# A message-passing kernel: edge groups of 125 with 12 targets in place of 250 with 24, and one of four source one-hots on ScalarE

## The chip, the cores and the metric

The kernel runs on one core of a Trainium2 chip. The core has five engines with a queue of instructions each: TensorE (PE, matmuls; its weight loads have a row of their own, PEld), VectorE (DVE), ScalarE (ACT), GpSimd (POOL) and SyncE (SP, which here only starts transfers). They wait for each other through semaphores. The metric is the time of one execution on the device in microseconds, as a median of several runs; one further execution is recorded by the profiler.

## The reference

The inputs are x of 1250 nodes with 1024 features, 40,000 edges (src, dst) sorted by target, two graph layers, and a mixture of eight experts. Cut to what matters:

```python
def sage_layer(h, src, dst, deg_inv, W_self, W_neigh, b):
    agg = segment_sum(h[src], dst, num_segments=N)
    return h @ W_self + (agg * deg_inv[:, None]) @ W_neigh + b

deg = segment_sum(ones, dst, N);  deg_inv = 1 / maximum(deg, 1)
h = relu(sage_layer(layernorm(x), ..., W_self0, W_neigh0, b0))
x = x + sage_layer(h, ..., W_self1, W_neigh1, b1)
x = x + ffn(layernorm(x))     # router, top 2 of 8 experts, weighted sum
```

The targets are drawn as 1250 u^2 with u uniform, so they are denser at low numbers.

## The kernel before

The sum over edges is a matrix product: C[s, t] is the number of edges from source s to target t, and agg = C^T h. C is kept on the chip as 10 blocks of 128 sources by 1250 targets (`C`, line 367, fp32r). Both layers multiply by it; its column sums are the degrees.

**How C is counted.** The 40,000 edges, in the order given, are cut into 160 groups of 250. As targets are sorted, a group has few different targets; the kernel assumes at most 24 (`WIN`), numbered from the group's first. A group is two subgroups of 125 edges (`GC, GP`), one edge on each partition. For a subgroup, a one-hot of the source's low seven bits is made on GpSimd (`ol`, line 413, 125 x 128), a one-hot of the pair (source block, target within the window) on VectorE (`oh`, line 420, 125 x 240), and a matmul of the two (line 423) counts the edges; the two subgroups of a group accumulate in PSUM. The 240 counts are then added on VectorE (line 442) to the ten block rows of C at the group's first target. That place is known only at run time: line 437 loads it into a VectorE register ahead of each addition, and register arithmetic makes an address of it (also recorded under line 442).

**Rows of groups.** Two groups (four subgroups) are a row; there are 80. `row_of_groups` makes the four `ol`, then four times `oh` and matmul into one PSUM tile (`cnt`, three buffers), and then, when more than two rows are open, `close_row` makes the two additions of the oldest. `oh` and `ol` have six buffers each. `make_keys` and `turn_keys` compute and transpose the numbers that the one-hots compare with; `turn_ranges` brings first and last target of each group to one partition; `verdict` tests that every group fits its window (if not, a general path runs after everything else, which these inputs don't take).

**What lies around it.** While C is counted, TensorE multiplies the normalised tokens by `W_self0` (`self_unit`, line 462, evicted by ScalarE on line 466) and by `W_neigh0` (`y_unit`, line 528; `split`, lines 393 and 394, evicts with one ScalarE copy and one VectorE subtraction). `some_groups(n)` puts n rows of groups between the units: 9 rows before the loop, 2, 4 and 4 before the three units of each of six blocks, 1 before each of ten y units, and the rest behind them. The first matmul that reads the finished C is line 553 (degrees); then come the products with C (line 564).

**What sets the order.** The opening (LayerNorm of six blocks, transposes, first units, keys) is written out by hand for VectorE, ScalarE and TensorE (`manual_schedule`). Elsewhere a planner simulates the engines and takes, for each, the earliest instruction in program order that is ready; `keep_in_program_order` pins an instruction behind the one traced before it on its engine. Once planned, each engine's queue is fixed, and its instructions start in that order.

Of the kernel before, what the change touches and what calls it, by code (L numbers as in the profile page):

```python
# [10 lines left out]
F32 = mybir.dt.float32  # L11
F32R = mybir.dt.float32r
F16 = mybir.dt.float16
# [7 lines left out]

P = 128
EPS = 1e-5
WIN = 24
GC, GP = 2, 125
LQ = 32


# [1 line left out]
def kernel(  # L30
# [28 lines left out]
    QW = D // 4  # L59
    NB = -(-N // P)  # L60
    NP = NB * P
    EG = GC * GP
    NGR = NE // EG
    R = NGR // 2
    WEXP = KD * H + KH * D
    NTILE = (2 * N) // P + E
    assert R * 2 * EG == NE and R <= P and 2 * NB * WIN <= 512 and N > WIN
    rows = [min(P, N - b * P) for b in range(NB)]

    step = -(-(N - 2 * P) // 4) * 2  # L70
# [72 lines left out]
    stt = nc.vector.scalar_tensor_tensor  # L143


    RE = 2 * EG
    assert 8 * RE <= 4000 and 3 * NGR <= 500 and 8480 + 6 * NGR <= 9440
# [16 lines left out]
    nc.vector.memset(eps, EPS)  # L164

    nc.scalar.activation(small.tile([P, 1], F32, name="rs"), eps, AF.Sqrt)
    ident = const.tile([P, P], F32, name="ident")
    make_identity(nc, ident)

# [27 lines left out]
    nc.scalar.dma_start(out=b0_p, in_=b0.rearrange("(k p) -> p k", p=P))  # L197


    ext = const.tile([R, 3, 2], F32, name="ext")  # L200
    base_i = const.tile([1, NGR], I32, name="base_i")

    keys = const.tile([GP, 2, 2 * GC, R], F32, name="keys")
# [4 lines left out]
    APART = 16  # L208
    assert APART * EG < 4096

    dst_halves = dst_f.rearrange("p (a n) -> p a n", a=2)

    def make_keys():

        nc.vector.tensor_reduce(ext[:, 0, :], dst_halves, AX.X, ALU.min)
        nc.vector.tensor_scalar(ext[:, 2, :], ext[:, 0, :], float(N - WIN), None, op0=ALU.min)
        nc.vector.tensor_scalar(hi_i, src_i, 7, None, op0=ALU.arith_shift_right)
        nc.vector.tensor_scalar(lo_i, src_i, P - 1, None, op0=ALU.bitwise_and)
        nc.vector.tensor_copy(hi_f, hi_i)
        nc.vector.tensor_copy(lo_f, lo_i)  # L220
        stt(key, hi_f, float(WIN), dst_f, op0=ALU.mult, op1=ALU.add)
        for i in range(2):
            part = key[:, i * EG : (i + 1) * EG]
            nc.vector.tensor_scalar(part, part, ext[:, 2, i : i + 1], None, op0=ALU.subtract)

    def turn_keys():
        for a, v in enumerate((key, lo_f)):
            ps = tpp.tile([P, 4, P], F32, name="tp")
            pf = ps.rearrange("p a b -> p (a b)")
            for c in range(2 * GC):  # L230
                nc.tensor.transpose(
                    pf[:GP, c * R : (c + 1) * R], v[:, c * GP : (c + 1) * GP], ident[:R, :R]
                )
            nc.scalar.copy(keys[:, a].rearrange("p c g -> p (c g)"), pf[:GP, : 2 * GC * R])

    def turn_ranges():

        nc.vector.tensor_reduce(ext[:, 1, :], dst_halves, AX.X, ALU.max)
        for a in (2, 0, 1):
            pe = tpp.tile([P, 4, P], F32, name="tp")  # L240
            for i in range(2):
                nc.tensor.transpose(pe[:1, i, :R], ext[:, a, i : i + 1], ident[:R, :R])
            nc.vector.tensor_copy(
                gx[:, a, :].rearrange("o (r i) -> o i r", i=2), pe[:1, :2, :R]
            )
            if a == 2:
                nc.vector.tensor_copy(base_i, gx[:, 2, :])

    def verdict():

        bad = L[:1, 8480 : 8480 + 6 * NGR].rearrange("o (a g) -> o a g", a=6)
        nc.vector.memset(bad, -1.0)
        stt(bad[:, 0, :], hi_, float(1 - WIN), lo_, op0=ALU.add, op1=ALU.subtract)
        nc.vector.tensor_tensor(bad[:, 1, : NGR - 1], lo_[:, : NGR - 1], lo_[:, 1:], ALU.subtract)
        nc.vector.tensor_tensor(bad[:, 2, : NGR - 1], hi_[:, : NGR - 1], hi_[:, 1:], ALU.subtract)
        stt(
            bad[:, 3, : NGR - APART], hi_[:, : NGR - APART], 1.0, lo_[:, APART:],
            op0=ALU.add, op1=ALU.subtract,
        )
# [97 lines left out]
    def gnn_windows():  # L357
# [26 lines left out]

        yh = yp.tile([P, NB, QW], F32R, name="yh")
        yl = yp.tile([P, NB, QW], F32R, name="yl")
        win = yp.tile([P, NB * WIN], F16, name="win")
        win_i = yp.tile([P, NB * WIN], I32, name="win_i")
        nc.gpsimd.iota(win_i, pattern=[[1, NB * WIN]], base=0, channel_multiplier=0)
# [18 lines left out]
        GW = NB * WIN  # L408

        def row_of_groups(r):  # L410
            ol = hot.tile([GP, 2 * GC, P], F16, name="ol")
            for c in range(2 * GC):
                nc.gpsimd.tensor_scalar(  # L413
                    ol[:, c, :], lane[:GP], keys[:, 1, c, r : r + 1], None, op0=ALU.is_equal
                )
            ps = pc.tile([P, 2, 256], F32, name="cnt")
            for i in range(2):
                for c in range(GC):
                    oh = hot.tile([GP, GW], F16, name="oh")
                    nc.vector.tensor_scalar(  # L420
                        oh, win[:GP], keys[:, 0, i * GC + c, r : r + 1], None, op0=ALU.is_equal
                    )
                    nc.tensor.matmul(  # L423
                        ps[:, i, :GW], ol[:, i * GC + c, :], oh,
                        start=(c == 0), stop=(c == GC - 1),
                    )
            open_rows.append((r, ps))
            if len(open_rows) > 2:
                close_row()

        open_rows = []

        def close_row():
            r, ps = open_rows.pop(0)
            for i in range(2):
                g = 2 * r + i
                at = nc.values_load(
                    base_i[0:1, g : g + 1], engines=(ENG.DVE,), min_val=0, max_val=N - WIN,
                    skip_runtime_bounds_check_because="cut at N - WIN, and a target is never below 0",
                )  # L440
                to = C[:, :, ds(at, WIN)]
                nc.vector.tensor_tensor(  # L442
                    to, to.bitcast(F32),
                    ps[:, i, :GW].rearrange("p (k w) -> p k w", k=NB), ALU.add,
                )

        groups = iter(range(R))

# [87 lines left out]
        for q in range(4):  # L536
            w_q = w_next
            w_next = load_q(w_neigh0, q + 1) if q < 3 else None
            for b in range(NB):
                if q == 0:  # L540
                    some_groups(1)
                y_unit(w_q, h0T, b, yh[: rows[b], b, :], yl[: rows[b], b, :])
            if q == 3:
                w_half = load_half(w_neigh1, 0)
            if q == 0:
                some_groups(R)
                while open_rows:
                    close_row()

                for c0, n in cchunks:  # L550
                    ps = mm.tile([P, 512], F32, name="ps")
                    for k in range(NB):
                        nc.tensor.matmul(
                            ps[:, :n], ones_r, C[:, k, c0 : c0 + n],
                            start=(k == 0), stop=(k == NB - 1),
                        )
                    nc.vector.tensor_scalar(dinv[:, c0 : c0 + n], ps[:, :n], 1.0, None, op0=ALU.max)
                    nc.vector.reciprocal(dinv[:, c0 : c0 + n], dinv[:, c0 : c0 + n])
# [1123 lines left out]
```

## Time and profile before

| | |
|---|---|
| median of 3 runs | 1146.44 us (1146.19 to 1147.84) |
| profiled execution, its own time | 1146.48 us |
| its span | 1144.3 us |
| granted TensorE clock, mean | 0.993 |
| TensorE busy | 1108.3 us |
| VectorE, GpSimd, ScalarE busy | 451.1, 331.7, 181.5 us |
| counting stage, first one-hot to the first matmul on the finished C | 31.64 to 234.62 us |

A group of instructions in the profile is one line, engine and operation: out<-in by tile names, partitions x elements, count, busy time and mean of one in ns; behind the bar the engine's idle time just before them and who ended it. In a row of stretches each engine has its busy time and in brackets the number of instructions. In a timeline a row is start, length, engine, line and operation, merged over neighbours. Register instructions (DVEq) are not counted as busy.

### The profile page before, as it was taken

The numbers are of one execution on the slowest core, as the hardware profiler recorded it, in microseconds if no ns is written. First come the engines' busy times: TensorE is split into PE (matmuls) and PEld (weight loads), VectorE is DVE, ScalarE is ACT, GpSimd is POOL, SyncE is SP. The second block draws the span as 40 slices with busy tenths as digits, with TensorE's granted clock in tenths as the row PEclk, the third lists the DMA queues.
The fourth block names the chain that finished last, engine by engine and source line by source line (L and its number), as shares of the span: only waits on it lengthen the run. The fifth ranks groups of instructions, "written<-read, shape, count | busy, mean of one in ns | idle before, by whom it ended". The sixth has DMA issues, their size and how long they took to land.

```text
span 1144.3 us, 13214 instructions
## 1 busy us (share of the span) xinstructions
PE 1108.3 (97%) x4775; PEld 791.2 (69%) x4775; DVE 451.1 (39%) x1129; ACT 181.5 (16%) x420; POOL 331.7 (29%) x438
## 2 busy tenths in 40 slices
PE   6999999999999999999999999999999989999994
PEld 4556556888888886887688778885444766666662
DVE  8777777761212154341224132555322542111110
ACT  5301000001111111100110000123011223222220
POOL 1899999800000000032003002342000013223221
PEclk9999999999999999999999999999999999999997
DMA  6110111010100021042004261335921435444542
GB/s 230 34 38 5 38 38 38 1 37 1 38 1 1 1 74 38 1 154 93 7 10 168 88 222 42 117 148 209 373 60 37 150 92 136 112 113 105 127 115 45
DMA packets 59330, 95.40 MB, mean 83 GB/s; under 512 B 8797, under 2 KB 35645, under 8 KB 59251
## 3 DMA queue, kind: packets, MB, share of 16 engines
q1 hardware_dynamic: 48400, 67.72, 17.3%
q0 software_dynamic: 7056, 23.88, 9.2%
q10 hardware_dynamic: 3798, 2.84, 0.8%
q8 instruction: 42, 0.69, 0.2%
q14 instruction: 34, 0.28, 0.1%
HBM read 68.76 MB, written 27.47 MB: 84 GB/s over the span
## 4 chain that ended last, share of the span: by engine, by line
PE 93%; DVE 2%; ACT 1%; DMA 1%; POOL 1%; issue 0%; ACTq 0%; DVEq 0%; POOLq 0%
PE ps L528 12%; PE ps L462 11%; PE psb L642 9%; PE ps L712 8%; PE ps L564 8%; PE ps L642 7%; PE ps L1516 7%; PE ps L1541 7%; PE ps L1188 5%; PE ps L629 5%; PE ps L1202 4%; PE cnt L423 3%; PE tp L1504 2%; PE ps L1141 2%; PE ps L1537 1%; PE tp L322 1%
## 5 line engine op out<-in xcount | busy, mean ns | idle before, releaser
L413 POOL TENSOR_SCALAR ol<-lane,keys 125x128 f16<-125x128 f16 x320 | 193.2, 622 | 27.6 <-DVE oh L420 27.6
L462 PE MATMUL ps<-h0T,L 128*128 128x498 f32 (+2 forms) x384 | 147.4, 518 | 0.2 <-ACT h0T L325 0.2
L528 PE MATMUL ps<-L,h0T 128*128 128x256 f32 (+1 forms) x640 | 142.0, 380 | 0.0
L708 POOL TENSOR_TENSOR L<-L 128x512 f32<-128x512 f32 (+1 forms) x20 | 31.4, 1576 | 375.1 <-DMA L<-in_L_gnn_b_dram 216.5
L528 PEld LDWEIGHTS ps<-L,h0T 128*128 128x128 f32 (+1 forms) x640 | 118.7, 188 | 17.7 <-issue 0.5
L420 DVE TENSOR_SCALAR oh<-win,keys 125x240 f16<-125x240 f16 x320 | 84.7, 322 | 32.7 <-PE cnt L423 31.1
L462 PEld LDWEIGHTS ps<-h0T,L 128*128 128x128 f32 x384 | 68.1, 192 | 38.3 <-issue 33.9
L1516 PE MATMUL ps<-xw,L 128*128 x368 | 84.9, 384 | 0.4 <-issue 0.4
L1541 PE MATMUL ps<-xw,L 128*128 x184 | 83.5, 597 | 0.1
L564 PE MATMUL ps<-C,yh 128*128 128x256 f32 (+2 forms) x240 | 81.9, 356 | 0.0
L564 PE MATMUL ps<-C,yl 128*128 128x256 f32 (+2 forms) x240 | 81.5, 354 | 0.0
L712 PE MATMUL ps<-zh,C 128*128 128x512 f32 (+1 forms) x200 | 79.6, 398 | 0.0
L712 PE MATMUL ps<-zl,C 128*128 128x512 f32 (+1 forms) x200 | 78.7, 393 | 0.0
L1516 PEld LDWEIGHTS ps<-xw,L 128*128 128x128 f32 x368 | 69.2, 193 | 10.3 <-issue 1.8
L1552 POOL DMA_INDIRECT out_dram<-L x23 | 36.3, 1579 | 133.5 <-ACT L L1505 87.9
L442 DVE TENSOR_TENSOR C<-C,cnt 128x240 f32 x160 | 64.3, 402 | 12.5 <-DVE oh L420 1.6
L1493 POOL DMA_INDIRECT L<-t_d,L x26 | 26.0, 1000 | 148.1 <-DVE L L141 127.8
L1541 PEld LDWEIGHTS ps<-xw,L 128*128 128x128 f32 x184 | 33.3, 190 | 35.3 <-issue 32.9
L423 PEld LDWEIGHTS <-ol 125*128 125x128 f16 x320 | 30.9, 97 | 36.7 <-POOL ol L413 20.0
L1549 DVE TENSOR_SCALAR L<-ps,L 128x512 f32<-128x512 f32 x23 | 17.3, 751 | 91.8 <-PE ps L1541 91.8
L394 DVE TENSOR_TENSOR yl<-ps,yh 128x256 fp32r<-128x256 f32 (+1 forms) x40 | 16.9, 424 | 92.1 <-ACT yh L393 92.1
L423 PE MATMUL cnt<-oh,ol 125*128 125x240 f16 x320 | 50.0, 266 | 2.6 <-POOL ol L413 2.1
(226 smaller groups left out, 1504.3 us busy)
## 6 DMA issues: line engine op xcount, KB each, us to landing
xw<-in_L_ffn_ew_dram SPq DMA_DIRECT2D x16, 1024.0 KB, 7.6
L<-in_x_dram SPq DMA_DIRECT2D x20, 256.0 KB, 2.8
v_d<-L SPq DMA_DIRECT2D x18, 256.0 KB, 2.0
xa<-v_d SPq DMA_DIRECT2D x18, 256.0 KB, 6.0
t_d<-L SPq DMA_DIRECT2D x9, 512.0 KB, 4.0
out_dram<-xa SPq DMA_DIRECT2D x9, 512.0 KB, 3.7
L<-in_L_gnn_W_self_dram SPq DMA_DIRECT2D x4, 1024.0 KB, 5.4
L<-in_L_gnn_W_neigh_dram SPq DMA_DIRECT2D x4, 1024.0 KB
```

The costliest lines, as they stand in the source:

```text
L413: nc.gpsimd.tensor_scalar(ol[:, c, :], lane[:GP], keys[:, 1, c, r : r + 1], None, op0=ALU.is_equal)
L420: nc.vector.tensor_scalar(oh, win[:GP], keys[:, 0, i * GC + c, r : r + 1], None, op0=ALU.is_equal)
L423: nc.tensor.matmul(ps[:, i, :GW], ol[:, i * GC + c, :], oh, start=(c == 0), stop=(c == GC - 1),)
L442: nc.vector.tensor_tensor(to, to.bitcast(F32), ps[:, i, :GW].rearrange("p (k w) -> p k w", k=NB), ALU.add,)
L462: nc.tensor.matmul(ps[:, :n], w[:, k, (d % 2) * P : (d % 2 + 1) * P], h0T[:, k, c0 : c0 + n], start=(k == 0), stop=(k == KD - 1),)
L528: nc.tensor.matmul(ps[:m, :QW], hT[:, k, blk(b)], w[:, k, :], start=(k == 0), stop=(k == KD - 1))
L564: nc.tensor.matmul(ps[:, :n], part[: rows[k], k, (d % 2) * P : (d % 2 + 1) * P], C[: rows[k], k, c0 : c0 + n], start=(k == 0 and part is y ...
L629: nc.tensor.matmul(ps[:m], hT1[:, k, blk(b)], w[:, k, :], start=(k == 0), stop=(k == KD - 1))
L642: nc.tensor.matmul(ps, rows_of(k), w[:, k, :], start=(first and k == 0), stop=(k == KB - 1), skip_group_check=not first,)
L712: nc.tensor.matmul(ps[:m], C[: rows[k], k, blk(b)], part[: rows[k], k, :], start=(k == 0 and part is yh), stop=(k == NB - 1 and part is yl),)
L1516: nc.tensor.matmul(ps[:, :H], xT[:, k, :], w1_all[:, ds(e, 1), k * H : (k + 1) * H], start=(k == 0), stop=(k == KD - 1),)
L1541: nc.tensor.matmul(ps, hT[:, q, :], w2_all[:, ds(e, 1), q * D + h * HALF : q * D + (h + 1) * HALF], start=False, stop=(q == KH - 1),)
```

## The change

- A group is 125 edges with at most 12 targets (`EG`, `WIN`); a row is four groups (`RG`), still 80 rows. The two subgroups no longer share a result: each of the four matmuls of a row writes 120 counts of its own, and there are 320 additions of 120 counts, each with its register load.
- `row_of_groups` makes three source one-hots on GpSimd; the fourth comes from ScalarE as relu(1 - |key - lane|) in two activations.
- Additions no longer follow a row in a block: after each one-hot and matmul, `add_group` makes one addition once eight groups are waiting. One-hots and additions are pinned in program order on VectorE.
- `ext`, `base_i` and `keys` move from the pool that lives throughout to one that is freed after the stage; the verdict's scratch is twice as long and lies over the edge words (4000 on) rather than behind the ranges. The ranges are 320 numbers instead of 160, so their turn needs four transposes where it had two.
- 16 matmuls of the identity with itself, whose result nobody reads, stand at the head of TensorE's order.
- Two rows instead of one precede the first y unit.

```diff
-WIN = 24
-GC, GP = 2, 125
+WIN = 12
+EG = 125
+RG = 4
...
-    R = NGR // 2
+    R = NGR // RG
...
-    RE = 2 * EG
+    RE = RG * EG
...
+    one_p = const.tile([P, 1], F32, name="one_p")
+    nc.vector.memset(one_p, 1.0)
...
-        for i in range(2):
+        for i in range(RG):
             part = key[:, i * EG : (i + 1) * EG]
             nc.vector.tensor_scalar(part, part, ext[:, 2, i : i + 1], None, op0=ALU.subtract)
...
         for a in (2, 0, 1):
             pe = tpp.tile([P, 4, P], F32, name="tp")
-            for i in range(2):
+            for i in range(RG):
                 nc.tensor.transpose(pe[:1, i, :R], ext[:, a, i : i + 1], ident[:R, :R])
...
-        bad = L[:1, 8480 : 8480 + 6 * NGR].rearrange("o (a g) -> o a g", a=6)
+        bad = L[:1, 4000 : 4000 + 6 * NGR].rearrange("o (a g) -> o a g", a=6)
...
         def row_of_groups(r):
-            ol = hot.tile([GP, 2 * GC, P], F16, name="ol")
-            for c in range(2 * GC):
-                nc.gpsimd.tensor_scalar(
-                    ol[:, c, :], lane[:GP], keys[:, 1, c, r : r + 1], None, op0=ALU.is_equal
-                )
-            ps = pc.tile([P, 2, 256], F32, name="cnt")
-            for i in range(2):
-                for c in range(GC):
-                    oh = hot.tile([GP, GW], F16, name="oh")
+            ol = hot.tile([EG, RG, P], F16, name="ol")
+            for i in range(RG):
+                k = keys[:, 1, i, r : r + 1]
+                if i < RG - 1:
+                    nc.gpsimd.tensor_scalar(ol[:, i, :], lane[:EG], k, None, op0=ALU.is_equal)
+                else:
+
+                    away = hot.tile([EG, P], F16, name="away")
+                    nc.scalar.activation(away, lane[:EG], AF.Abs, scale=-1.0, bias=k)
+                    nc.scalar.activation(ol[:, i, :], away, AF.Relu, scale=-1.0, bias=one_p[:EG])
+            ps = pc.tile([P, RG, P], F32, name="cnt")
+            for i in range(RG):
+                oh = hot.tile([EG, GW], F16, name="oh")
+                tc.keep_in_program_order(
                     nc.vector.tensor_scalar(
-                        oh, win[:GP], keys[:, 0, i * GC + c, r : r + 1], None, op0=ALU.is_equal
+                        oh, win[:EG], keys[:, 0, i, r : r + 1], None, op0=ALU.is_equal
                     )
-                    nc.tensor.matmul(
-                        ps[:, i, :GW], ol[:, i * GC + c, :], oh,
-                        start=(c == 0), stop=(c == GC - 1),
-                    )
-            open_rows.append((r, ps))
-            if len(open_rows) > 2:
-                close_row()
...
+                )
+                nc.tensor.matmul(ps[:, i, :GW], ol[:, i, :], oh, start=True, stop=True)
+
+                if len(to_add) >= 2 * RG:
+                    add_group()
+            to_add.extend((r, ps, i) for i in range(RG))
+
+        to_add = []
+
+        def add_group():
+            r, ps, i = to_add.pop(0)
+            g = RG * r + i
+            at = nc.values_load(
+                base_i[0:1, g : g + 1], engines=(ENG.DVE,), min_val=0, max_val=N - WIN,
...
+            to = C[:, :, ds(at, WIN)]
+            tc.keep_in_program_order(
                 nc.vector.tensor_tensor(
                     to, to.bitcast(F32),
                     ps[:, i, :GW].rearrange("p (k w) -> p k w", k=NB), ALU.add,
                 )
+            )
...
+            idle = mm.tile([P, 512], F32, name="ps")
+            for _ in range(16):
+                nc.tensor.matmul(idle[:, :P], ident, ident, start=True, stop=True)
             step(0, 0, 1, 0, 1)
...
-                    some_groups(1)
+                    some_groups(2 if b == 0 else 1)
...
-                while open_rows:
-                    close_row()
+                while to_add:
+                    add_group()
```

More of the change, by code (lines that the diff above doesn't have):

```diff
@@ L61 @@
     NP = NB * P
-    EG = GC * GP
     NGR = NE // EG
-    R = NGR // 2
+    R = NGR // RG
     WEXP = KD * H + KH * D
     NTILE = (2 * N) // P + E
-    assert R * 2 * EG == NE and R <= P and 2 * NB * WIN <= 512 and N > WIN
+    assert R * RG * EG == NE and R <= P and RG * NB * WIN <= 512 and N > WIN
     rows = [min(P, N - b * P) for b in range(NB)]
@@ L143 @@
     stt = nc.vector.scalar_tensor_tensor
-    RE = 2 * EG
-    assert 8 * RE <= 4000 and 3 * NGR <= 500 and 8480 + 6 * NGR <= 9440
+    RE = RG * EG
+    assert 8 * RE <= 4000 and 3 * NGR <= 1440 and 6 * NGR <= 4 * RE
     edge = L[:R, 4000:8000].rearrange("p (a n) -> p a n", n=RE)
@@ L197 @@
     nc.scalar.dma_start(out=b0_p, in_=b0.rearrange("(k p) -> p k", p=P))
-    ext = const.tile([R, 3, 2], F32, name="ext")
-    base_i = const.tile([1, NGR], I32, name="base_i")
-    keys = const.tile([GP, 2, 2 * GC, R], F32, name="keys")
+    ext = base_i = keys = None
     worst = const.tile([1, 1], F32, name="worst")
@@ L207 @@
     lo_, hi_ = gx[:, 0, :], gx[:, 1, :]
-    APART = 16
+    APART = 32
     assert APART * EG < 4096
-    dst_halves = dst_f.rearrange("p (a n) -> p a n", a=2)
+    dst_groups = dst_f.rearrange("p (a n) -> p a n", a=RG)
     def make_keys():
-        nc.vector.tensor_reduce(ext[:, 0, :], dst_halves, AX.X, ALU.min)
+        nc.vector.tensor_reduce(ext[:, 0, :], dst_groups, AX.X, ALU.min)
         nc.vector.tensor_scalar(ext[:, 2, :], ext[:, 0, :], float(N - WIN), None, op0=ALU.min)
@@ L229, in turn_keys @@
             pf = ps.rearrange("p a b -> p (a b)")
-            for c in range(2 * GC):
+            for c in range(RG):
                 nc.tensor.transpose(
-                    pf[:GP, c * R : (c + 1) * R], v[:, c * GP : (c + 1) * GP], ident[:R, :R]
+                    pf[:EG, c * R : (c + 1) * R], v[:, c * EG : (c + 1) * EG], ident[:R, :R]
                 )
-            nc.scalar.copy(keys[:, a].rearrange("p c g -> p (c g)"), pf[:GP, : 2 * GC * R])
+            nc.scalar.copy(keys[:, a].rearrange("p c g -> p (c g)"), pf[:EG, : RG * R])
     def turn_ranges():
-        nc.vector.tensor_reduce(ext[:, 1, :], dst_halves, AX.X, ALU.max)
+        nc.vector.tensor_reduce(ext[:, 1, :], dst_groups, AX.X, ALU.max)
         for a in (2, 0, 1):
             pe = tpp.tile([P, 4, P], F32, name="tp")
-            for i in range(2):
+            for i in range(RG):
                 nc.tensor.transpose(pe[:1, i, :R], ext[:, a, i : i + 1], ident[:R, :R])
             nc.vector.tensor_copy(
-                gx[:, a, :].rearrange("o (r i) -> o i r", i=2), pe[:1, :2, :R]
+                gx[:, a, :].rearrange("o (r i) -> o i r", i=RG), pe[:1, :, :R]
             )
@@ L386, in gnn_windows @@
         yl = yp.tile([P, NB, QW], F32R, name="yl")
+        nonlocal ext, base_i, keys
+        ext = yp.tile([R, 3, RG], F32, name="ext")
+        base_i = yp.tile([1, NGR], I32, name="base_i")
+        keys = yp.tile([EG, 2, RG, R], F32, name="keys")
         win = yp.tile([P, NB * WIN], F16, name="win")
@@ L410, in row_of_groups @@
         def row_of_groups(r):
-            ol = hot.tile([GP, 2 * GC, P], F16, name="ol")
-            for c in range(2 * GC):
-                nc.gpsimd.tensor_scalar(
-                    ol[:, c, :], lane[:GP], keys[:, 1, c, r : r + 1], None, op0=ALU.is_equal
-                )
-            ps = pc.tile([P, 2, 256], F32, name="cnt")
-            for i in range(2):
-                for c in range(GC):
-                    oh = hot.tile([GP, GW], F16, name="oh")
-                    nc.vector.tensor_scalar(
-                        oh, win[:GP], keys[:, 0, i * GC + c, r : r + 1], None, op0=ALU.is_equal
-                    )
-                    nc.tensor.matmul(
-                        ps[:, i, :GW], ol[:, i * GC + c, :], oh,
-                        start=(c == 0), stop=(c == GC - 1),
-                    )
@@ L427, in row_of_groups @@
-            open_rows.append((r, ps))
-            if len(open_rows) > 2:
-                close_row()
[L431 to L441, printed above, removed]
+            ol = hot.tile([EG, RG, P], F16, name="ol")
@@ new lines, in row_of_groups @@
+            for i in range(RG):
+                oh = hot.tile([EG, GW], F16, name="oh")
+                tc.keep_in_program_order(
+                    nc.vector.tensor_scalar(
+                        oh, win[:EG], keys[:, 0, i, r : r + 1], None, op0=ALU.is_equal
+                    )
+                )
+                nc.tensor.matmul(ps[:, i, :GW], ol[:, i, :], oh, start=True, stop=True)
+                if len(to_add) >= 2 * RG:
+                    add_group()
+            to_add.extend((r, ps, i) for i in range(RG))
@@ L442, in close_row @@
+        to_add = []
[4 more added lines that the diff above has]
+                base_i[0:1, g : g + 1], engines=(ENG.DVE,), min_val=0, max_val=N - WIN,
+                skip_runtime_bounds_check_because="cut at N - WIN, and a target is never below 0",
+            )
+            to = C[:, :, ds(at, WIN)]
+            tc.keep_in_program_order(
                 nc.vector.tensor_tensor(
@@ L445, in close_row @@
                 )
+            )
         groups = iter(range(R))
```

## The prediction

> **What bounds the kernel now.** I read the page first, then busy time by stretch, the groups, the waits and the timeline of the stretch that the change touches.
>
> ```profile
> PE 1108.3 (97%) x4775; PEld 791.2 (69%) x4775; DVE 451.1 (39%) x1129; ACT 181.5 (16%) x420; POOL 331.7 (29%) x438
> ```
>
> TensorE is busy 97% of the span, so a microsecond counts if it comes off TensorE or makes TensorE wait. The stretches of the counting stage:
>
> ```profile
> core 0: us, PE busy (x) PEld busy (x) DVE busy (x) ACT busy (x) POOL busy (x), PEclk, DMA share, GB/s
> 32.00:60.00 28.00, 25.54 (x114) 13.77 (x113) 20.54 (x72) 8.90 (x16) 27.86 (x43) 1.00 0.00 1
> 120.00:150.00 30.00, 30.00 (x119) 16.32 (x118) 22.81 (x76) 2.50 (x4) 30.00 (x52) 1.00 0.00 1
> 225.00:240.00 15.00, 13.40 (x71) 11.04 (x70) 9.71 (x23) 1.02 (x3) 0.32 (x1) 1.00 0.22 71
> ```
>
> GpSimd has no gap from 32 to 225 us, and TensorE hardly any, since it does weight products between the counts. The groups:
>
> ```profile
> L413 POOL TENSOR_SCALAR ol<-lane,keys 125x128 f16<-125x128 f16 x320 | 193.2, 622 | 27.6 <-DVE oh L420 27.6
> ...
> L420 DVE TENSOR_SCALAR oh<-win,keys 125x240 f16<-125x240 f16 x320 | 84.7, 322 | 32.7 <-PE cnt L423 31.1
> ...
> L442 DVE TENSOR_TENSOR C<-C,cnt 128x240 f32 x160 | 64.3, 402 | 12.5 <-DVE oh L420 1.6
> ...
> L423 PE MATMUL cnt<-oh,ol 125*128 125x240 f16 x320 | 50.0, 266 | 2.6 <-POOL ol L413 2.1
> ```
>
> What TensorE loses by waiting is small: 2.1 us for GpSimd's one-hots, and 1.6 us at the end of the stage for the last addition. VectorE waits 31.1 us for count matmuls; it has room. The end of the stage on TensorE:
>
> ```profile
> 232.45 0.57 PE L423 MATMUL cnt<-oh,ol 125*128 125x240 f16 x4
> 234.62 6.00 PE L553 MATMUL ps<-C,ones_r 128*128 128x256 f32 x30 [1.60 <-DVE C L442]
> ```
>
> The first matmul on the finished counts, at 234.62, is the gate: everything later follows it. The forecast is where this gate goes. The profiled execution took 1146.48 us for its span of 1144.3 (2.2 us lie around it), and the median shown is 1146.44, so a shift of the span is taken as a shift of the median.
>
> **TensorE's part.** The 320 count matmuls stay 320, with 120 columns for 240. A burst of four lasts 0.57 us with 0.27 for the last, so they follow each other by 0.102 us. The nearest short row, also 16-bit with new weights for each:
>
> ```profile
> 951.56 0.84 PE L1359 MATMUL tp<-L 128*128 128x69 bf16 x20
> ```
>
> Twenty of 69 columns in 0.84 us, the last one 0.20 long: 0.034 apart. Between 69 and 240 columns that is 0.40 ns a column, so 120 columns need 0.054, and 320 x 0.048 = 15.4 us come off. The Trainium skill ("TensorE: Matmul & The Clock Gate", Back-to-back issue gap) speaks against this: streams of weight load and matmul hold some 81 ns at 128 columns[...]; by it the gain is 320 x 0.021 = 6.7 us. I take the row, since its weights change each time as here. With the 2.6 us of waits gone, 0.6 us for six more small transposes of the ranges (0.1 each) and 1.2 us from the clock (next), TensorE alone could be at the gate at 233.0 (its last count's end) - 15.4 - 2.6 - 1.2 + 0.6 = 214.4.
>
> **The 16 idle matmuls** run between the identity (1.5 us) and the first transposes (9.1 us), in TensorE's idle time. Now the first eight transposes take 1.94 us and a later eight 1.03; the first weight unit 4.75 us, the next 3.62. A unit at full clock is worth 1.1 us, and TensorE and ScalarE form the chain from there to the keys at 31.6, so I give it 1.2 (bounds: 0 if LayerNorm on VectorE sets the pace, 2 if the transposes count too). Each of the 16 is two records; at the cold unit's 0.3 us a record of twice the columns, they end by 7 us or, at full cold price, 11 us, which would cost 2 us.
>
> **GpSimd and ScalarE.** GpSimd makes 240 of 320 one-hots: 240 x 0.622 = 149 us, free by about 181; it stops being near the limit. ScalarE makes 80 with two activations of 128 elements each: from the evictions (0.474 us for 256, 0.676 for 498) 0.37 us each, 160 x 0.37 = 59 us in a stage where it is busy 2.5 of 30. Nothing on the path, since six buffers let it run ahead; an eviction queued behind it comes 0.7 us later, and three accumulators cover that. Table loads stand only at three later lines and at the start; should Abs need one, 1.28 us twice a row would make ScalarE the bound (I give it 2 in 100).
>
> **VectorE's part decides.** One-hots: 320 of half the width, 0.03 to 0.05 us less each. Additions: 320 instead of 160, each half as wide: 240 elements take 0.405, 256 in the splits 0.42, ten elements 0.15, so about 0.28. Together 320 x (0.28 + 0.28) = 179 us by durations, less by overlap (one-hots start 0.19 apart, and an instruction starts 0.08 before an addition has ended): about 0.40 us a group, 128 us. But each addition reads its place first:
>
> ```profile
> L437 DVEq TENSOR_LOAD <-base_i x160: 297/303/551, 37.6 to 233.7; - x160
> ...
> L442 DVEq FUSED_REGOPS  x160: 69/69/69, 38.3 to 234.0; - x160
> ```
>
> These are no busy time, but they hold VectorE's queue. Look at two additions in a row:
>
> ```profile
> 142.10 0.93 DVE L442 TENSOR_TENSOR C<-C,cnt 128x240 f32 x2
> 142.94 1.21 DVE L420 TENSOR_SCALAR oh<-win,keys 125x240 f16<-125x240 f16 x4
> 144.20 0.93 DVE L442 TENSOR_TENSOR C<-C,cnt 128x240 f32 x2
> ```
>
> Two take 0.93 with the second 0.40 long: 0.53 apart, though one lasts 0.40. The records say why: load starts 0.03 after the addition, register arithmetic 0.38 later, the addition 0.12 after that. That does not shrink with the width. Where a one-hot stood between two additions and the queue ran freely, loads started at 80.430 and 80.993: 0.563 apart. The load runs while the one-hot computes, which is what the alternation buys: four one-hots and then four additions would cost 4 x 0.526 and the one-hots besides. So VectorE's queue needs 309 x 0.563 + 11 x 0.526 = 180 us for the groups. It starts about 35.6 (first load now 37.6; 1.2 from the clock, and the first addition stands after one one-hot of row 2, not four, less 0.5 for wider range copies). Other VectorE work in the stage is 13 us busy, and the verdict's rows double (its reduction 1.14 to 2.2, its fill of minus ones no longer at 5.8 us but behind the keys, 0.86 to 1.6); much of it lies in the 0.16 us a group that the queue leaves the engine, so 10 us (bounds 5 and 18). 35.6 + 180 + 10 = 226 on VectorE against 214 on TensorE: the bound of this stage changes over to VectorE.
>
> **What is queued behind.** An addition is the last reader of a row's PSUM bank, and three banks exist. In the new order a row's third one-hot is followed by the last addition of three rows before, and only then may the row's first matmul run. I put 2 us on what this and the small mismatches cost (bounds 0 and 24, the slower rival). Splits of the first y units (VectorE, 0.42 us) stand in the same queue and free TensorE's accumulators; 0 to 5 us, I take 1. TensorE, short of work near the end, may drop its clock: the skill's page (The HAM clock gate) has half speed after about 3.4 idle us. Before, TensorE is never idle that long here, so there is no row; price 0 to 3.4 us, and I take 0, because counts still come every 2.3 us. 226 + 2 + 1 = 229 for the gate, and 1146.4 - (234.6 - 229) = 1140.8, about 1141.
>
> **Rivals.**
> 1. TensorE stays the bound: VectorE's queue overlaps better than 0.563, or its other work hides. Gate at 214 to 218: 1126 to 1130. For it: VectorE shows 31 us of waits. Against: 0.526 is the least seen between two loads. 10 in 100.
> 2. The y units wait. VectorE at 2.25 us a row gets through 71 rows at about 204; if the splits keep their place behind those rows, three accumulators fill and seven units of 3.46 + 0.22 follow: gate at 204.5 + 25.7 = 230, and TensorE idle before it, so 3 of cold clock: 233 and 1145, within 0.2% of no change. Against: in the profile of before a split is done within a row of its unit. 17 in 100.
> 3. Slower: the PSUM bank is released too late. Place: the row's first count matmul behind the addition in the third slot. Price: if TensorE is then inside a product (0.42 us) and VectorE runs out of its six one-hot buffers, 0.3 us a row is lost, 80 x 0.3 = 24 us: gate at 250, 1162. It decides from (234.6 - 226) / 80 = 0.11 us a row. For it: VectorE already waits for counts 35 times. Against: the buffers allow one-hots four slots (2.25 us) beyond the release. 25 in 100.
> That narrower windows don't shorten the matmuls at all (weights bind) would put TensorE at 230: within rival 2.
>
> **How the numbers follow.** The likeliest case, VectorE's queue at 0.563, has 48 in 100 and its own range 1133 to 1144. A measurement tells about 0.2% (2.3 us) from nothing. Faster: 48 + 10 - 3 for its upper edge = 55. Same: most of rival 2 and a little of the others, 18. Slower: rival 3 and its milder forms, 27. The range leaves out the lower half of rival 1 and the worst of 3: 1129 to 1159.
>
> **What would show it.** Right: count matmuls in bursts at 0.05 us; loads of line 437's successor about 0.56 apart through the stage; GpSimd with gaps; waits of TensorE for VectorE's additions or one-hots some 10 us in sum; gate at 225 to 231. Wrong: register loads under 0.53 apart, no TensorE waits (rival 1); long TensorE waits for splits from about 185 (2); VectorE waiting for counts every row (3); table loads in the stage.

## The result and the profile after

The changed kernel takes 1204.3 us (median of 4 runs, 1204.05 to 1205.09) beside 1146.99 for the kernel before in the same comparison: a ratio of 1.0501, 95% interval 1.0483 to 1.0519. It is 57 us slower, where 1141 and at most 1159 were forecast. The span of the profiled execution grew from 1144.3 to 1202.7 us.

The gate, the first matmul on the finished counts, moved from 234.62 to 290.20 us, which is 55.6 of the 58.4 us. Another 2.3 lie in the thirty matmuls of ones just behind it (8.3 us for 6.0, the first of them at half clock). So the counting stage holds nearly all of the loss. First the page's busy times of the changed kernel:

```profile
PE 1116.2 (93%) x4813; PEld 794.9 (66%) x4813; DVE 469.6 (39%) x1292; ACT 242.1 (20%) x580; POOL 280.9 (23%) x358
```

TensorE was busy 97% of the span and is now busy 93%; its idle time grew from 36 to 87 us. Busy time by stretch of the changed kernel (columns as in the line of names: busy time and number of instructions of each engine, then the granted clock of TensorE):

```profile
core 0: us, PE busy (x) PEld busy (x) DVE busy (x) ACT busy (x) POOL busy (x), PEclk, DMA share, GB/s
60.00:90.00 30.00, 30.00 (x112) 16.85 (x111) 18.75 (x69) 8.49 (x19) 13.49 (x23) 1.00 0.13 36
90.00:120.00 30.00, 30.00 (x113) 15.89 (x112) 17.34 (x72) 10.07 (x23) 15.84 (x27) 1.00 0.00 1
200.00:250.00 50.00, 12.28 (x88) 7.34 (x88) 42.81 (x178) 17.37 (x44) 38.78 (x67) 0.50 0.00 0
252.00:282.00 30.00, 29.56 (x144) 24.26 (x144) 16.75 (x73) 4.15 (x11) 7.14 (x12) 0.90 0.01 2
```

Two engines take turns at standing still. From 60 to 120 us TensorE is full and VectorE works only 0.6 of the time. From 200 to 250 it is the other way round: VectorE's queue never waits for counts (busy 0.86 of the time; its register loads are not counted), TensorE is busy for 12 of 50 us at half clock. From 252 on TensorE is full again. The timeline of TensorE shows why (start, duration, and in brackets the idle time before; a product is two records). First the kernel before:

```profile
141.18 0.58 PE L423 MATMUL cnt<-oh,ol 125*128 125x240 f16 x4
141.59 1.84 PE L462 MATMUL ps<-h0T,L 128*128 128x498 f32 x4
143.27 0.57 PE L423 MATMUL cnt<-oh,ol 125*128 125x240 f16 x4
```

Then the changed kernel:

```profile
100.30 3.21 PE L471 MATMUL ps<-h0T,L 128*128 128x496 f32 x12
103.35 0.37 PE L433 MATMUL cnt<-oh,ol 125*128 125x120 f16 x4
103.56 4.02 PE L471 MATMUL ps<-h0T,L 128*128 128x256 f32 x12
107.42 0.38 PE L433 MATMUL cnt<-oh,ol 125*128 125x120 f16 x4
...
192.04 3.67 PE L541 MATMUL ps<-L,h0T 128*128 128x256 f32 x16
195.56 0.38 PE L433 MATMUL cnt<-oh,ol 125*128 125x120 f16 x4
...
228.65 0.56 PE L433 MATMUL cnt<-oh,ol 125*128 125x120 f16 x4 [1.67 <-DVE C L450]
230.88 0.56 PE L433 MATMUL cnt<-oh,ol 125*128 125x120 f16 x4 [1.67 <-DVE C L450]
...
252.09 5.49 PE L541 MATMUL ps<-L,h0T 128*128 128x256 f32 x12 [0.25 <-DVE yl L398]
...
290.20 6.07 PE L566 MATMUL ps<-C,ones_r 128*128 128x256 f32 x20 [5.99 <-DVE C L450]
```

While there are weight products, TensorE's queue places 2.5 to 3.6 us of them between two rows of counts, so a row mostly comes every 2.8 to 3.7 us (from 70.0 to 195.6 us 36 times, 3.49 in the mean with one pause). Before, two products, 1.7 us, mostly stood between rows from 100 us on. At 197 us products and three y units are done, and only 47 of the 80 rows. Then 24 rows follow with nothing between them, most of them 2.23 us apart, to 251 us. Only after these come the other y units, with a row each, 3.7 us apart, and at the end 6 us of waiting for the last eleven additions.

The order of VectorE's queue holds the y units back. Its timeline in the changed kernel:

```profile
250.86 0.28 DVE L450 TENSOR_TENSOR C<-C,cnt 128x120 f32 x1
251.05 0.32 DVE L429 TENSOR_SCALAR oh<-win,keys 125x120 f16<-125x120 f16 x1
251.42 0.28 DVE L450 TENSOR_TENSOR C<-C,cnt 128x120 f32 x1
251.62 0.42 DVE L398 TENSOR_TENSOR yl<-ps,yh 128x256 fp32r<-128x256 f32 x1
```

The split at 251.62 is the first of all. Its y unit was ready at about 189 us; it stands behind the additions of the bare rows. Three accumulators were full meanwhile. (Before, the first split ran at 203.2.) The waits of the changed kernel from 26 to 310 us, engine and line, what it waited for, and sum, times and longest:

```profile
DVE oh L429 <- PE cnt L433: 48.0, 44, 2.7
PE cnt L433 <- DVE C L450: 40.9, 24, 2.2
PE ps L566 <- DVE C L450: 6.0, 1, 6.0
```

VectorE waited 48.0 us for TensorE's counts, 38.3 of it up to 196 us; TensorE waited 40.9 us for VectorE's additions, 39.3 of it after that. A smaller loss lies in between: at the routing constants (small VectorE work for a later stage) TensorE stands still for 7.1 us in three pauses from 137.6 to 146.6 us, the last of them for the DMA of weights, and its clock is at half from 141.9 to 152.1; the kernel before shows no such pause at the constants. Each engine by itself is as fast as forecast, which the groups show:

```profile
L419 POOL TENSOR_SCALAR ol<-lane,keys 125x128 f16<-125x128 f16 x240 | 142.3, 610 | 120.6 <-PE cnt L433 90.2
L429 DVE TENSOR_SCALAR oh<-win,keys 125x120 f16<-125x120 f16 x320 | 85.7, 274 | 48.6 <-PE cnt L433 48.0
L450 DVE TENSOR_TENSOR C<-C,cnt 128x120 f32 x320 | 89.5, 280 | 36.0 <-DVE oh L429 12.3
L424 ACT ACTIVATE ol<-away,one_p 125x128 f16<-125x128 f16 x80 | 31.6, 399 | 113.8 <-PE cnt L433 113.8
```

An addition of 120 elements takes 0.280 us (0.28 worked out), an activation 0.399 (0.37), GpSimd is busy 142 us (149), and no table is loaded in the stage.

### The profile page after: what moved, and what is told of

Same layout as the page of the kernel before. It is cut to its first block, busy times and chain, and to the rows that moved or that the text cites. A ratio compares the mean times of both kernels' runs of the same rounds, so it can differ in the third digit from the quotient of the medians.

```text
span 1202.7 us, 13989 instructions
## 1 busy us (share of the span) xinstructions
PE 1116.2 (93%) x4813; PEld 794.9 (66%) x4813; DVE 469.6 (39%) x1292; ACT 242.1 (20%) x580; POOL 280.9 (23%) x358
## 4 chain that ended last, share of the span: by engine, by line
PE 87%; DVE 6%; DMA 2%; DVEq 1%; ACT 1%; issue 1%; POOL 0%; ACTq 0%; POOLq 0%; SPq 0%
PE ps L541 12%; PE ps L471 11%; PE psb L655 9%; PE ps L725 8%; PE ps L577 8%; PE ps L655 7%; PE ps L1529 6%; PE ps L1554 6%; PE ps L1201 5%; PE ps L642 5%; PE ps L1215 3%; DVE C L450 3%; PE tp L1517 2%; PE ps L1154 2%; DVE oh L429 1%; DMA b_p<-in_L_gnn_b_dram 1%
## 5 line engine op out<-in xcount | busy, mean ns | idle before, releaser
L419 POOL TENSOR_SCALAR ol<-lane,keys 125x128 f16<-125x128 f16 x240 | 142.3, 610 | 120.6 <-PE cnt L433 90.2
L429 DVE TENSOR_SCALAR oh<-win,keys 125x120 f16<-125x120 f16 x320 | 85.7, 274 | 48.6 <-PE cnt L433 48.0
L471 PEld LDWEIGHTS ps<-h0T,L 128*128 128x128 f32 x384 | 71.3, 195 | 49.7 <-issue 41.3
L450 DVE TENSOR_TENSOR C<-C,cnt 128x120 f32 x320 | 89.5, 280 | 36.0 <-DVE oh L429 12.3
L433 PE MATMUL cnt<-oh,ol 125*128 125x120 f16 x320 | 36.6, 241 | 48.5 <-DVE C L450 40.9
L433 PEld LDWEIGHTS <-ol 125*128 125x128 f16 x320 | 25.4, 107 | 75.7 <-POOL ol L419 51.0
L424 ACT ACTIVATE ol<-away,one_p 125x128 f16<-125x128 f16 x80 | 31.6, 399 | 113.8 <-PE cnt L433 113.8
```

The lines of the kernel that those rows point to most:

```text
L419: nc.gpsimd.tensor_scalar(ol[:, i, :], lane[:EG], k, None, op0=ALU.is_equal)
L429: nc.vector.tensor_scalar(oh, win[:EG], keys[:, 0, i, r : r + 1], None, op0=ALU.is_equal)
L433: nc.tensor.matmul(ps[:, i, :GW], ol[:, i, :], oh, start=True, stop=True)
L450: nc.vector.tensor_tensor(to, to.bitcast(F32), ps[:, i, :GW].rearrange("p (k w) -> p k w", k=NB), ALU.add,)
L471: nc.tensor.matmul(ps[:, :n], w[:, k, (d % 2) * P : (d % 2 + 1) * P], h0T[:, k, c0 : c0 + n], start=(k == 0), stop=(k == KD - 1),)
```

## The experiments

The working theory after this reading: **the order of the queues**. TensorE's order was laid with rows too far apart while products lasted; VectorE idled, and what it had not done came afterwards, with TensorE idle. The rivals: **VectorE's queue as such** (a register load for each of 320 additions is too much work wherever the rows stand), and **the pins**. The parts that have nothing to do with it, the idle matmuls and ScalarE's share, were run alone. A ratio is always to the kernel before in the same comparison.

**Without the pins.** Both `keep_in_program_order` around the one-hot and the addition are taken away.

> The changed kernel without the two pins on VectorE; the planner then places one-hots and additions itself. Theory of TensorE's order (the planner spaces the rows of count matmuls some 3.4 us apart while weight products last, so that only 46 of 80 rows are counted when they run out): the planner lays the same spacing, so 1195 to 1210. Theory of the pins (alternation is what makes VectorE's queue slow): 1150 to 1165, with row starts 2.3 us or less apart from 70 us on.

1205.1 us, ratio 1.0505 (1.0489 to 1.0521); gate 290.0; rows 3.49 apart to 195.7 us, then 2.23. The first one-hot starts at 31.7 instead of 38.8 us, for it no longer stands behind the ranges' copies, and those 7 us are worth nothing at the end. The pins are out as a cause.

**Rows spread over the products.** The edit pins only TensorE's order; the planner lays the other queues around it.

```
-                nc.tensor.matmul(ps[:, i, :GW], ol[:, i, :], oh, start=True, stop=True)
+                ins = nc.tensor.matmul(ps[:, i, :GW], ol[:, i, :], oh, start=True, stop=True)
+                if 9 <= r < 69:
+                    tc.keep_in_program_order(ins)
...
+                if between:                      # in self_unit, after the product
+                    tc.keep_in_program_order(ins)
+                    if (k + 1) % (KD // between) == 0:
+                        some_groups(1)
...
-                    some_groups(4 if c else 2)
-                    self_unit(w_q, d, c)
+                    self_unit(w_q, d, c, between=4 if c else 2)
```

> The changed kernel with one thing more: the count matmuls of rows 9 to 68 and the products are pinned in program order on TensorE, a row after every two or four products' weights, so that rows stand 2.1 us of products apart. Nothing of VectorE's work changes. Theory of TensorE's order: rows follow at VectorE's own pace of 2.25 us from the start, the stretch of bare rows from 197 to 251 us goes, the first matmul on the finished counts at 230 to 237 us, 1143 to 1152 in all. Theory of VectorE's queue as such (each addition costs more beside products than I worked out): rows stay over 3 us apart, 1190 to 1205.

1168.1 us, ratio 1.0175 (1.0159 to 1.0191): 36 of the 57 us come back by order alone. TensorE's timeline of this kernel:

```profile
118.16 0.64 PE L433 MATMUL cnt<-oh,ol 125*128 125x120 f16 x4 [6.78 <-DVE oh L429]
...
150.16 1.89 PE L473 MATMUL ps<-h0T,L 128*128 128x498 f32 x4
152.15 0.44 PE L433 MATMUL cnt<-oh,ol 125*128 125x120 f16 x4
152.42 1.88 PE L473 MATMUL ps<-h0T,L 128*128 128x496 f32 x4
154.37 0.37 PE L433 MATMUL cnt<-oh,ol 125*128 125x120 f16 x4
...
252.17 2.08 PE L571 MATMUL ps<-C,ones_r 128*128 128x256 f32 x8 [6.00 <-DVE C L452]
```

Rows now follow at 2.23 us from 72 us on, VectorE's own pace, and the bare rows are gone. So the order theory had the larger cause right. But its number, 1143 to 1152, was missed: the gate is at 252.2, not 230 to 237. TensorE could do a row with two products in 1.94 us (it does for four rows behind the pause) and is held to 2.23 or more for 46 rows; the y units, with a row every 3.7 us, then keep TensorE busy until the wait for the last additions. There is also one pause of 6.8 us at 111 us: the routing constants, some 16 small instructions and a wait for a DMA of 1.5 us, stand in VectorE's queue between two rows. Part of the loss is therefore VectorE's own.

**One register load a row.**

```
-            at = nc.values_load(
-                base_i[0:1, g : g + 1], engines=(ENG.DVE,), min_val=0, max_val=N - WIN,
+            if i == 0:
+                _, places[:] = nc.values_load_multi_w_load_instructions(
+                    base_i[0:1, g : g + RG], engines=(ENG.DVE,), min_val=0, max_val=N - WIN,
...
+            at = places[i]
```

> The changed kernel with one register load for the four places of a row instead of four loads; all else as it was, the order the planner's. A row of VectorE should take 0.56 + 3 x 0.40 to 0.45 = 1.8 to 1.9 us for 2.25. Theory of TensorE's order: rows are still placed three products (2.9 us) apart, fewer stay for the end, 1165 to 1185. Theory of VectorE's queue as such: the gain is that of 240 loads at 0.12 to 0.16 us, 29 to 38 us: 1166 to 1175; so time alone does not tell these apart, the spacing of the rows does (2.9 against 1.9).

1164.7 us, ratio 1.0149 (1.0132 to 1.0166). Timeline of TensorE in this kernel:

```profile
162.03 0.37 PE L433 MATMUL cnt<-oh,ol 125*128 125x120 f16 x4
162.25 2.73 PE L473 MATMUL ps<-h0T,L 128*128 128x498 f32 x6
164.81 0.37 PE L433 MATMUL cnt<-oh,ol 125*128 125x120 f16 x4
...
195.87 0.56 PE L433 MATMUL cnt<-oh,ol 125*128 125x120 f16 x4 [1.00 <-DVE C L452]
197.44 0.56 PE L433 MATMUL cnt<-oh,ol 125*128 125x120 f16 x4 [1.01 <-DVE C L452]
199.17 0.56 PE L433 MATMUL cnt<-oh,ol 125*128 125x120 f16 x4 [1.17 <-DVE C L452]
```

Two things in one view. The bare rows stand 1.62 us apart (195.87 to 200.73, three rows) for 2.23: three register loads less are 0.61 us, 0.20 a load. And the theory of order is confirmed by the spacing: among products most rows are 2.4 to 2.8 us apart although VectorE could do one in 1.62, with one stretch of 17 us (117.5 to 134.6) without any row, and bare rows remain (17 pauses of about 1.1 us from 188 to 215 us).

**Both edits.**

> The two edits together: rows of count matmuls two products apart on TensorE, and one register load for a row's four places. VectorE's row (1.9) is then no longer than TensorE's (two products and a burst, 1.87 to 1.9), so neither waits for the other except at the routing constants (6.8 us of idle TensorE in the kernel with spread rows): gate near 236, 1144 to 1151. If VectorE's rows stay at 2.25, 1160 or more.

1146.7 us, ratio 0.9994 (0.9986 to 1.0003): no longer slower than the kernel before. The gate is at 232.45. Its timeline of TensorE:

```profile
111.30 0.56 PE L433 MATMUL cnt<-oh,ol 125*128 125x120 f16 x4 [6.22 <-DVE C L454]
...
150.93 0.38 PE L433 MATMUL cnt<-oh,ol 125*128 125x120 f16 x4
151.14 1.95 PE L475 MATMUL ps<-h0T,L 128*128 128x256 f32 x8
152.93 0.37 PE L433 MATMUL cnt<-oh,ol 125*128 125x120 f16 x4
```

Rows stand 1.94 to 2.0 us apart with TensorE full between them; the pause for the routing constants is still there. Of the 55.6 us lost at the gate 38.0 come back by spreading the rows (290.2 to 252.2), and then 19.7 by taking three of four register loads (252.2 to 232.5). The two do not simply add: the loads alone gave 40.1, a part of which is order as well, since the planner then lays rows closer.

**No register loads at all.** `to = C[:, :, :WIN]`: every group is added at the first 12 targets, so the counts are not the reference's.

> The changed kernel with the place of each addition fixed: no register load and no register arithmetic, every group is added at the first 12 targets (the counts it leaves are not the reference's). VectorE's pair of a one-hot and an addition then takes 0.40 us, a row 1.6. My prediction put TensorE alone at 214.4 us at the gate, which with the idle matmuls' loss instead of a gain (+2.5) is 217: 1127 to 1132. If something else than register loads, and the order that goes with them, holds the stage (ScalarE's one-hots, PSUM banks, pins), it stays above 1150.

1139.1 us, ratio 0.993 (0.9914 to 0.9947); gate 225.6. One-hot and addition take 0.40 us a pair, as worked out, and the waits of TensorE in the stage are down to 0.3 us and the last 4.4. Nothing else in the change holds the stage then: ScalarE's one-hots, the banks and the pins are all still there. (This edit does not divide the cost between the loads and the order, for the planner lays the rows anew here too: 1.96 us apart in the mean from 63.9 to 183.7 us, where it was 3.49 with four loads a row and 2.8 with one.) The time missed what was expected by 7 us: the wait for the last additions, 4.4, had been left out, and TensorE's last work ahead of the gate ends at 221.2 where 217 was expected. From its 25th to its last product this kernel spends 146.4 us, of which 276 counts at 0.053 are 14.6; before it is 153.1 with 249 counts at 0.103: so what is left for the products is 131.8 and 127.5, 4.3 us longer, though no wait is recorded. Most of it lies behind the bursts: from start to start, the first record of a product takes 0.475 us at 496 columns when it stands behind a burst of narrow counts, 0.425 behind wide ones, and 0.416 amid products in both kernels; 69 bursts make 3.5 us of it. Why a narrow burst slows what follows it is open.

**The idle matmuls alone,** added to the kernel before.

> The kernel before with one part of the change, the 16 idle matmuls. The prediction gave them 1.2 us: 1145.8 to 1146 for 1147, the keys 1.2 us earlier than in the kernel before. The reading of the trace of the changed kernel gives another answer: the first unit's eviction ended at the same time as before (it waits for its bias), and a pause of 2.4 us then put the clock back to half, so the keys came 1.3 us later. By that reading this kernel is 0 to 1.3 us slower than the kernel before.

1148.8 us, ratio 1.0008 (0.9999 to 1.0017): no gain; the one profile says a loss, the gate is at 235.87 for 234.62. TensorE's timeline of this kernel:

```profile
8.98 1.09 PE L322 MATMUL tp<-ident,L 128*128 128x128 f32 x8 [1.76 <-DVE L L339]
...
24.58 1.15 PE L322 MATMUL tp<-ident,L 128*128 128x128 f32 x8 [2.57 <-ACT h0T L325]
25.92 1.97 PE L322 MATMUL tp<-ident,L 128*128 128x128 f32 x8 [0.19 <-ACT h0T L325]
27.71 4.41 PE L462 MATMUL ps<-h0T,L 128*128 128x498 f32 x8
```

The first transposes do take 1.09 instead of 1.94 us. But the work ends in a wait for VectorE and ScalarE, the pause before 24.58 grows from 1.35 to 2.57, and after it TensorE is at half speed again: 1.97 for 1.14 and 4.41 for 3.61. The keys come 1.3 us late.

**ScalarE's share alone,** added to the kernel before: the diff's `away` and `Relu` for `c == 3`.

> The kernel before with one part of the change, ScalarE's share: of a row's four source one-hots ScalarE makes the fourth, by two activations (the keys and places move to another buffer to make room). My step: 160 activations of 0.40 us beside the path, GpSimd at 80 x 3 x 0.62 = 149 us, TensorE's 2.1 us of waits for GpSimd gone: 1144 to 1146 for 1147. If ScalarE's share harms (evictions late behind it), 1149 or more.

1144.0 us, ratio 0.9971 (0.9961 to 0.9982): a gain of 3 us, as worked out. The gate is at 231.35, and of 2.1 us of waiting for GpSimd's one-hots 0.2 is left. This part of the change is good in itself.

**One register load a row, in the kernel before,** for its two additions.

> The kernel before with one register load for the two places of a row: 80 loads go from a VectorE that has room. If a register load costs only where VectorE sets the pace, no change within 0.2% (1145 to 1149.5), apart from where the planner then puts the rows; if it costs everywhere, 80 x 0.12 to 0.38 = 10 to 30 us less.

1157.8 us, ratio 1.0088 (1.0075 to 1.0101), slower: neither answer. The gate is at 243.95. TensorE's timeline of this kernel:

```profile
165.29 5.18 PE L462 MATMUL ps<-h0T,L 128*128 128x498 f32 x12
170.32 0.78 PE L423 MATMUL cnt<-oh,ol 125*128 125x240 f16 x6
170.93 1.00 PE L462 MATMUL ps<-h0T,L 128*128 128x496 f32 x2
171.77 0.78 PE L423 MATMUL cnt<-oh,ol 125*128 125x240 f16 x6
172.39 1.00 PE L462 MATMUL ps<-h0T,L 128*128 128x496 f32 x2
173.23 0.43 PE L423 MATMUL cnt<-oh,ol 125*128 125x240 f16 x2
174.00 0.28 PE L423 MATMUL cnt<-oh,ol 125*128 125x240 f16 x1 [0.34 <-POOL ol L413]
```

With fewer instructions on VectorE the rows were laid in clusters, four within some 4 us and then six products. GpSimd needs 2.47 us a row (4 x 0.618) and can't follow: TensorE's waits that end on its one-hots grow from 2.1 to 6.5 us for matmuls and from 20.0 to 28.1 for weight loads. Measured from start to start, so with short waits as well, the counts inside the bursts lose 8.4 us more than before, which is most of the 9.3 at the gate. So an edit that takes work from an engine with room cost 10 us through the order of another's queue.

**Towards a faster version.** Four kernels on top of "both edits", all without the idle matmuls.

With the routing constants moved into the second quarter of the y units:

> The two edits together, without the idle matmuls, and with the routing constants (small VectorE work with a wait for a DMA) made in the second quarter of the y units, after the gate. If the pause of 6.8 us of TensorE in the kernel with spread rows comes from these constants, another 7 us go, and 1.3 us for the idle matmuls: 1135 to 1143. If the pause only moves to the y units, 1142 to 1150.

1109.6 us, but this is no gain to be had: the constants are staged in a stretch of SBUF that by then holds the first layer's last outputs, so part of these is overwritten and the work after the gate isn't the same. Only its gate can be read: 222.1 us, with no pause at 105 us. That is 10.3 us earlier than with both edits, of which some 1.3 belong to the idle matmuls that are left out here. So the constants cost about 9 us: the pause of 6.2 and the half clock behind it, from 109.9 to 116.7 us.

With no row close behind the constants (the first row after them comes after eight products), and two rows ahead of the second y unit as well:

> The changed kernel with rows spread and one register load a row, without the idle matmuls, and with the rows moved away from the routing constants: after these, eight products' weights come before the next row, so that TensorE has 7 us of products while VectorE makes the constants. If the pause of 6.2 us of TensorE comes from them, gate near 225 for 232.4, 1136 to 1142; if TensorE then waits at another place, 1142 to 1147.

1143.7 us, ratio 0.9971 (0.9959 to 0.9982); gate 227.7. The pause shrank from 6.2 to 4.0 us and did not go, so the number was missed by 2 us.

With no row at all in that unit, and two rows ahead of each of the first four y units:

> The kernel with evenly placed rows and two edits more: no row in the unit after the routing constants, and two rows ahead of each of the first four y units and none ahead of the last, so that the last additions are made while TensorE still has a y unit. If the wait for the last additions (4.65 us) and the half clock after it (1.9 us) are what the alternation costs at the end, both go, with 2 to 4 us of the pause at 105 us: 1133 to 1139, gate 217 to 222. If rows ahead of y units now wait for VectorE instead, 1139 to 1144.

1143.6 us, ratio 0.9952 (0.9939 to 0.9966): faster than both kernels, and the lowest ratio of those that do the whole work, though its interval overlaps those of the last kernel and of ScalarE's share alone. The wait at the end did not go: 4.86 us. The last row was meant to stand ahead of the last but one y unit; the planner put it four matmuls ahead of the end.

So the y units and their rows were pinned as well:

> The last kernel left its wait of 4.9 us for the last additions: among the y units TensorE's order was still the planner's, which put the last rows behind most of the last unit. Here the rows and the y units of the first quarter are pinned on TensorE as well, so that the last row stands two y units ahead of the end. If the end wait and the half clock behind it then go (4.9 + 2.5 us) and no other wait comes, 1136 to 1139 beside 1148; if TensorE waits for VectorE at the pairs of rows instead, up to 4 us of it come back, 1139 to 1143.

1178.3 us, ratio 1.0264 (1.0248 to 1.0281), far outside what was expected. VectorE's timeline of this kernel:

```profile
193.72 0.28 DVE L454 TENSOR_TENSOR C<-C,cnt 128x120 f32 x1
200.64 0.42 DVE L398 TENSOR_TENSOR yl<-ps,yh 128x256 fp32r<-128x256 f32 x1 [6.63 <-ACT yh L397]
```

VectorE stops for 6.6 us at a split whose y unit TensorE is still computing; behind the split stand the additions that free the banks; and TensorE's next row of counts waits for these (mostly 2.06 us, with half clock in the y units between). The two queues run in lockstep, 51 us of VectorE's time at splits in all, and the gate is at 263.8. It is the mechanism of the changed kernel's end with the roles exchanged.

## Why the prediction was wrong, step by step

- **VectorE's queue per group, 0.563 us:** right. The bare rows stand 2.23 us apart, 0.557 a group. (The least between two loads in the kernel before was 0.513, not 0.526; nothing hangs on it.)
- **Its start at 35.6 us:** 4 us off. The first load is at 39.8, because the first one-hot, pinned, stands behind the ranges' copies. Without the pins it is at 38.0 and the gate unchanged.
- **The sum "35.6 + 180 + 10 = 226 on VectorE against 214 on TensorE: the bound of this stage changes over to VectorE":** this is the step that failed. It adds up each engine's work and takes the larger sum, as if the larger engine never waited for the smaller. Measured: 39.8 + 178 + 48.0 of waiting for counts = 266, and other work and small waits make up the 24 to the gate at 290. A sum is the time only if the other queue feeds this engine at its pace from the start, and TensorE's order did so at 3.49 us a row where VectorE needs 2.23. I took the order of before (two products a row) for granted, though the planner lays it anew for the changed kernel; why it laid the rows so far apart, no run shows. With rows two products apart the gate was still at 252 and not 229: VectorE set the pace among the products (2.23 us a row), and TensorE set it among the y units (3.7 us a row), so neither engine's sum was the time.
- **"I put 2 us on what this and the small mismatches cost":** the term for the PSUM bank is what was mis-sized. TensorE's waits on additions are 40.9 us, beyond the upper bound of 24 too; they are no small mismatch but the release of a bank at VectorE's pace, with nothing between the rows to fill the time.
- **Rival 2** ("The y units wait": "three accumulators fill and seven units" follow) is what happened, and its chain can be followed in the timeline. Its size was wrong by its start: VectorE reached the first split at 251.6, not 204; 38 us of waiting for counts and the start 4 us late lie ahead of it. From 252 on the y units and rows at 3.7 us (to 284) and the 6.0 us at the end follow. What was held against it, that before "a split is done within a row of its unit", was misread: the first three y units of the kernel before end at 196.0, 200.3 and 204.2 us and their splits start at 203.2, 205.8 and 207.8, up to three rows late; only from the fourth on is it so.
- **Rival 3** had the right sign and the wrong place: the PSUM bank does decide, but after the products, not during them.
- **TensorE's part, "15.4 us come off":** mis-sized by 3 us. Inside a burst the counts start 0.053 us apart (0.054 worked out), and from the first count of a burst to the next product it was 0.411 us and is 0.211, which would be 80 x 0.200 = 16.0. But the product behind a burst takes 0.05 longer than before, which the prediction had not priced: 80 x 0.15 = 12 us. The 81 ns of the Trainium skill ("TensorE: Matmul & The Clock Gate", Back-to-back issue gap) do not hold here: 0.068 us a count, when the delay of the product behind is put to the four counts.
- **The idle matmuls, 1.2 us:** no gain, and wrong in sign by the profiles, +1.3 at the gate (the times alone, at a ratio of 0.9999 to 1.0017, do not tell a loss from nothing). The unit was shorter, but the chain there runs through VectorE and ScalarE, and the pause that opened lowered the clock again.
- **GpSimd and ScalarE:** right, and shown alone to be worth 3 us.
- **The end, "309 x 0.563 + 11 x 0.526":** the eleven last additions were counted as VectorE's work. TensorE waits for them, 6.0 us, and pays 2.3 more at half clock, for which the prediction took 0 (bound 3.4).

## What to carry to other kernels

Two engines that feed each other through a few buffers take the larger of their sums only if the work of both is spread alike over the stage; so look at the order of the bound engine's partner, per step of the loop, before adding up. Where a planner lays that order, any edit that changes the price of one instruction lays it anew for all engines: here the same edit (fewer register loads) gave 40 us in one kernel and cost 10 in another. And an instruction that frees a buffer should not stand in its queue behind work that waits for the very engine that needs the buffer next.

## What the runs showed of the hardware

- The clock fell after shorter pauses than thought. A pause of 1.60 us at the gate left it at 1.00 (before). One of 2.09 us (one load a row, in the kernel before) was followed by half clock from about 244 to 247 us, one of 6.0 us (changed kernel) by half clock to 295. But one of 2.08 us at 22.2 us in the kernel with "no row close behind the constants" left it at 1.00, so the length of the pause alone does not decide. From the last matmul to the drop it was from 2.1 us (one load a row, in the kernel before) to 5.0 us (both edits); the Trainium skill ("TensorE: Matmul & The Clock Gate", The HAM clock gate) has an idle window of about 3.4 us, which the pause of 2.09 does not fill.
- Thin work does not keep the clock up: with a burst of four counts (0.56 us) every 2.23 us it stood at 0.50 from 200 to 250 us of the changed kernel.
- The granted clock in the profile's rows does not show the cold start: in the kernel before it reads 1.00 ahead of 15 us while eight transposes take 1.94 us, and 1.03 later.
- A register load that feeds an addition's address costs VectorE's queue 0.20 us a time, beyond what hides behind a one-hot, at no busy time at all.
- A burst of four narrow counts (120 columns) slows the product behind it by 0.05 us more than a burst of wide ones (240): its first record takes 0.475 for 0.425 us at 496 columns, 0.275 for 0.225 at 256.
